# GpSimd's pauses between transfers left out from run 0B on, in a two-layer mixture-of-experts kernel

## The chip, the cores and the metric

The kernel runs on one core of one Trainium2 chip. The core has five engines with an instruction stream each: TensorE (PE in the profile, with PEld for its weight loads), VectorE (DVE), ScalarE (ACT), GpSimd (POOL) and SyncE (SP, which only starts transfers). What is measured is the device time of one execution in microseconds, lower is better. The same program is run several times and the median is taken.

## The reference, cut to what matters

2048 tokens (two sequences of 1024) of 256 numbers pass six layers, each added to x. The layers are a mixture of experts L0 (8 experts, 2 for each token, hidden width 176, and one shared expert), a time mix and a channel mix, the same L0 again, a mixture L1 (32 experts, 6 for each token, hidden width 96, and a shared expert), an attention whose sum runs over a whole sequence, and L1 again:

```
x = x + 0.5 * L0_ffn(layernorm(x))
x = x + L0_attn(layernorm(x))
x = x + 0.5 * L0_ffn(layernorm(x))
x = x + 0.5 * L1_ffn(layernorm(x))
x = x + L1_attn(layernorm(x))
x = x + 0.5 * L1_ffn(layernorm(x))

def _L1_ffn_ref(...):
    scores = jax.nn.sigmoid(x @ gate_w)
    topk_w, topk_i = jax.lax.top_k(scores, TOP_K)        # 6 of 32
    topk_w = topk_w / (jnp.sum(topk_w, axis=-1, keepdims=True) + 1e-20)
    ...
    act = jax.nn.silu(g) * u
    routed = jnp.einsum('tef,efd,te->td', act, wd, combine)
    shared = jax.nn.silu(x @ sg) * (x @ su) @ sd
    return routed + shared

def _L1_attn_ref(X, W_in, b_in, W_out, b_out):
    ...
    A = jnp.sum(feature_map(K) * V, axis=-2)             # over all 1024 tokens of a sequence
    Y = A[:, None, :] * Q
    ...
    return Y + X
```

## The kernel before, in words

**The mixture of experts.** The tokens stay in SBUF as 16 tiles of 128. A mixture does not run every expert on every token. For groups of four tiles it normalizes and scores the tokens (`prep`), and works out a slot for each pair of token and expert, so that the pairs of one expert fill whole blocks of 128 slots (`plan`). GpSimd then writes the normalized rows to their slots in DRAM: `scatter`, line 566, one indirect transfer of 128 rows for each tile and each choice (`xs`). Each block is loaded by SyncE (`fetch`, line 733), transposed, multiplied with its expert's weights (lines 764 and 781) and stored (`outward`, line 790, `ys`). Then GpSimd fetches each token's results back: `gather`, line 801, one indirect transfer for each tile and choice into one of eight buffers `yk`, and DVE adds it to x with its weight (`add_back`, line 813). A gather of a group waits for the stores of all blocks that the group can have (55 of them for the first group of a half, all of them for the second). A load waits for all scatters of its run.

**The order of the second half.** L1 runs on half A (tiles 0 to 7, the first sequence) and on half B (tiles 8 to 15), once before the attention and once after it, so there are four runs of blocks: 0A, 0B, 1A, 1B. Each has 68 blocks that are always there and up to 11 more under a condition. Each run has 48 scatters and 48 gathers. The attention over half A, with the gathers of 0A ahead of it and `prep`, `plan` and the scatters of 1A behind it, is written in between the blocks of 0B; for half B the same begins with the gathers of 0B. Shared experts (`shared`) fill places where no block is ready.

**The planner.** Each engine takes its instructions in a fixed order, so the order must be written out. `Clock` is a small planner that runs while the kernel is being built. Blocks advance its time (`BLOCK`, 1.41 us for a block of L1), and threads for gathers, scatters and attention (`clock.begin`) are resumed when their due time has come, whereupon they write out their next instructions. GpSimd has a clock of its own, `clock.pool`: each indirect transfer adds `CALL` = 1.27 us to it (line 317), and the next one is not written out before that time (`call`). Two threads that want GpSimd at one time are served by rank; gathers go ahead of scatters.

**The pauses.** After each third transfer, `called` (line 315) calls `pause` (line 325), as long as `pauses["on"]` is true. A pause is five memsets of a spare tile on GpSimd (lines 330 and 333), tied into order between the third transfer and the next one, and it adds `PAUSE` = 1.4 us to `clock.pool`. With the flag false, only the order is kept: the third transfer takes the memset's part as the one that the next transfers must follow (lines 322 and 323). In the kernel before, the flag becomes false at line 1515, when all blocks of 1B have been written out.

Of the kernel before, what the change touches and what calls it, by code (L numbers as in the profile page):

```python
# [55 lines left out]
def macaron_kernel(ctx: ExitStack, tc: tile.TileContext, a: dict, out: bass.AP):  # L56
# [248 lines left out]
    pauses = {"on": True}  # L305
# [806 lines left out]
    def wait(done):  # L1112
        while not done():
            yield clock.now + 1.0
# [171 lines left out]
    def all_of(part):  # L1286
        for us in part:
            clock.run(us)
# [36 lines left out]
    def pieces_of(part):  # L1325

        return dict(step=lambda: next(part, None), fetch_ahead=lambda: None)
# [103 lines left out]
    def second_pass(h):  # L1431

        added, result = set(), {}
        clock.begin(0, given_rows(m1[h], range(2), added))

        yield from wait(lambda: h in summed)
        yield from attend(h, moe_pool, added, result)
        m2[h] = half(
            1,
            h,  # L1440
            given=result["given"],
            out=out[HT * h * P : (HT * h + HT) * P, :],
        )
        for g in range(2):
            with behind_blocks():
                for t in range(BT * g, BT * g + BT):
                    result["out_of"](t)
            yield clock.spent(7.0, 8.0)
            yield from onward(m2[h], g, ready2[h])
        with behind_blocks():  # L1450
            m2[h]["owners"]()
            m2[h]["weights"](0)
        yield clock.now

    def sends(m, planned, sent, h, rank):
        for g in range(2):
            yield from wait(lambda: g in planned[h])
            yield from m[h]["scatter"](g, rank)
            sent[h].add(g)
# [36 lines left out]
    settle(lambda: 1 in sent1[1])  # L1496
    clock.begin(3, second_pass(1))
    clock.begin(2, sends(m2, ready2, sent2, 1, 2))
    part = m1[1]["shared"](0, HT)
    all_of(m1[1]["blocks"](lambda: pieces_of(part)))  # L1500
    all_of(part)
# [10 lines left out]
    clock.begin(5, given_rows(m2[1], range(2), done[1], 5))  # L1512
    part = m2[1]["shared"](0, HT)
    all_of(m2[1]["blocks"](lambda: pieces_of(part)))
    pauses["on"] = False
    all_of(part)
    settle(lambda: 1 in done[0], lambda: 1 in done[1])

# [52 lines left out]
```

## Time and profile before

| | |
|---|---|
| median of 7 runs | 1448.41 us (1445.52 to 1455.32) |
| the profiled execution | 1449.62 us |
| its span, first to last instruction | 1447.8 us |
| granted TensorE clock, mean | 0.898 |
| busy: PE, DVE, ACT, POOL | 1261.5, 735.2, 622.4, 667.8 us |
| pauses (memsets of line 330) | 157 |
| blocks of 0A, first and last `pg` matmul | 735.7 to 848.2 us |
| blocks of 0B | 849.3 to 1024.6 us |
| blocks of 1A | 1162.4 to 1272.0 us |
| blocks of 1B | 1272.9 to 1382.3 us |
| gathers of 0A, 0B, 1A, 1B, first and last start | 840.0 to 938.5, 986.2 to 1098.2, 1262.6 to 1358.3, 1372.9 to 1438.8 us |
| scatters of 1A, 1B | 1024.8 to 1156.4, 1157.7 to 1233.5 us |

The span is one execution as the hardware profiler recorded it. A line of the timeline gives the start in microseconds from the span's start, the duration, the engine, the line of the kernel, the operation and its tiles, and in brackets how long the engine had been idle before and what ended that idle time. In a table of stretches, each engine's busy time stands beside the number of its instructions; PEclk is the clock that the throttle granted to TensorE, as a share of full speed, and the DMA share is the mean busy share of the 16 DMA engines. A row of waits gives who waited for whom, the total in us, how often, and the longest.

### The profile page before, as it was taken

Reading aid. Unit: us, or ns where it says so; the run is one execution under the profiler, and the core shown is the slowest. Engines: PE = TensorE matmul, PEld = TensorE weight load, DVE = VectorE, ACT = ScalarE, POOL = GpSimd, SP = SyncE. Lnnn points to the kernel's source line nnn. Section 1 sums busy time; section 2 is a strip of 40 time slices with the busy share of each in tenths; the row PEclk is TensorE's granted clock in tenths of the full one; section 3 lists DMA queues with packets and bytes.
Section 4 is the critical chain, followed back from the end, with each engine's and each line's share of the span. In section 5 each row is a group of like instructions: output and inputs, shape, how many; then the busy total and the mean of one; then the engine's idle time right before and its main releaser. Section 6 shows DMA issues by size and latency. Waiting matters only on the chain. (4 is left out here: it accounts for less than half of the span.)

```text
span 1447.8 us, 23152 instructions
## 1 busy us (share of the span) xinstructions
PE 1261.5 (87%) x6100; PEld 967.2 (67%) x6100; DVE 735.2 (51%) x2507; ACT 622.4 (43%) x1671; POOL 667.8 (46%) x1346
## 2 busy tenths in 40 slices
PE   6599889889999789999979998988898799999970
PEld 4577657456666667766758987767655678977850
DVE  5333445856552432456454446764587354455653
ACT  4023553478664223442434545443323154544520
POOL 1630532001110550367777355505667777165475
PEclk9589889889999679989989999997789699999995
DMA  9723422990001823433667776533322267677743
GB/s 286 231 74 105 139 77 77 310 317 1 0 0 41 213 80 96 146 99 113 182 200 245 223 213 200 164 99 99 110 60 77 83 199 250 202 223 231 237 131 105
DMA packets 195170, 214.94 MB, mean 148 GB/s; under 512 B 40892, under 2 KB 178012, under 8 KB 195036
## 3 DMA queue, kind: packets, MB, share of 16 engines
q1 hardware_dynamic: 170460, 146.22, 32.8%
q0 software_dynamic: 24576, 67.14, 15.2%
q8 instruction: 59, 0.97, 0.3%
q14 instruction: 75, 0.61, 0.2%
HBM read 103.04 MB, written 110.23 MB: 147 GB/s over the span
## 5 line engine op out<-in xcount | busy, mean ns | idle before, releaser
L801 POOL DMA_INDIRECT yk_L<-ys_L,idx_L x64 | 62.3, 973 | 186.6 <-DMA ys_L<-yb_L 123.0
L333 POOL MEMSET still<- 128x96 f32 x628 | 112.7, 179 | 36.1
L764 PE MATMUL pg_L_b<-L0gu,xbT_L 128*128 x312 | 110.4, 479 | 0.0
L566 POOL DMA_INDIRECT xs_L<-xn_L,idx_L x64 | 62.0, 969 | 74.6 <-DMA xs_L<-zero 28.9
L659 PE MATMUL pg_L<-L0sgu,xTs_L 128*128 128x352 f32 x256 | 89.6, 484 | 2.6 <-DVE h_L L650 2.6
L801 POOL DMA_INDIRECT yk_L_0B<-ys_B,idx_L_0B x48 | 49.1, 1022 | 73.8 <-DMA xb_L_0B<-xs_B 46.7
L781 PE MATMUL py_L_b<-L0down,hT_L_b 88*128 x312 | 82.0, 385 | 0.0
L801 POOL DMA_INDIRECT yk_L_0A<-ys_A,idx_L_0A x48 | 46.2, 962 | 63.0 <-DMA xb_L_0A<-xs_A 28.0
L801 POOL DMA_INDIRECT yk_L_1A<-ys_A,idx_L_1A x48 | 46.0, 959 | 60.8 <-DMA ys_A<-yb_L_1A 28.1
L781 PEld LDWEIGHTS py_L_b<-L0down,hT_L_b 88*128 88x128 f32 x312 | 59.7, 194 | 20.0 <-issue 1.0
L764 PEld LDWEIGHTS pg_L_b<-L0gu,xbT_L 128*128 128x128 f32 x312 | 56.5, 199 | 20.1 <-issue 3.0
L650 DVE TENSOR_TENSOR h_L_b<-g_L_b,pg_L_b 128x176 f32<-128x176 f32 x78 | 26.3, 337 | 83.9 <-ACT g_L_b L649 72.0
L983 PE MATMUL pkk_cm<-mk_cm,w_WkeyT 128*128 128x512 f32 x128 | 62.7, 622 | 5.2 <-DVE mk_cm L975 3.5
L659 PEld LDWEIGHTS pg_L<-L0sgu,xTs_L 128*128 128x128 f32 x256 | 47.9, 199 | 25.4 <-DVE h_L L650 4.3
L764 PE MATMUL pg_L_0B_b<-L1gu,xbT_L_0B 128*128 x272 | 59.6, 345 | 2.4 <-DVEq L906 1.7
L801 POOL DMA_INDIRECT yk_L_1B<-ys_B,idx_L_1B x48 | 46.4, 966 | 29.3 <-DMA ys_B<-yb_L_1B 13.4
L764 PE MATMUL pg_L_1B_b<-L1gu,xbT_L_1B 128*128 x272 | 57.4, 334 | 2.9 <-ACT xbT_L_1B L746 1.4
L764 PE MATMUL pg_L_0A_b<-L1gu,xbT_L_0A 128*128 x272 | 57.6, 336 | 2.2 <-ACT g_L_0A_b L649 0.8
L995 PE MATMUL pkv_cm<-w_WvalT,sk_cm 128*128 128x256 f32 x256 | 58.0, 379 | 0.1
L764 PE MATMUL pg_L_1A_b<-L1gu,xbT_L_1A 128*128 x272 | 57.5, 335 | 0.3 <-DVE m_L_1B L193 0.2
L995 PEld LDWEIGHTS pkv_cm<-w_WvalT,sk_cm 128*128 128x128 f32 x256 | 48.3, 190 | 12.0 <-issue 5.0
L649 ACT ACTIVATE g_L_b<-pg_L_b 128x176 f32<-128x176 f32 x78 | 24.8, 318 | 73.2 <-PE pg_L_b L764 61.6
(639 smaller groups left out, 3387.0 us busy)
## 6 DMA issues: line engine op xcount, KB each, us to landing
xs_A<-zero SPq DMA_DIRECT2D x1, 10112.0 KB
xs_B<-zero SPq DMA_DIRECT2D x1, 10112.0 KB
xb_L<-xs_L SPq DMA_DIRECT2D x78, 128.0 KB
ys_L<-yb_L SPq DMA_DIRECT2D x78, 128.0 KB
xb_L_0A<-xs_A SPq DMA_DIRECT2D x68, 128.0 KB
ys_A<-yb_L_0A SPq DMA_DIRECT2D x68, 128.0 KB
xb_L_0B<-xs_B SPq DMA_DIRECT2D x68, 128.0 KB
ys_B<-yb_L_0B SPq DMA_DIRECT2D x68, 128.0 KB
```

The costliest lines, as they stand in the source:

```text
L333: d = nc.gpsimd.memset(still, 0.0)
L566: d = nc.gpsimd.indirect_dma_start(out=xs, out_offset=bass.IndirectOffsetOnAxis(ap=idx[:, t, k : k + 1], axis=0), in_=sent[g][t - BT * g], ...
L649: nc.scalar.activation(g, pg[:, 0:width], AF.Silu)
L650: nc.vector.tensor_tensor(dst, g, pg[:, width : 2 * width], ALU.mult)
L659: nc.tensor.matmul(pg, xbT[:, c, i * P : (i + 1) * P], w["sgu"][:, c, u, :, :].rearrange("p z w -> p (z w)"), start=(c == 0), stop=(c == D ...
L764: nc.tensor.matmul(pg, xbT[:, c, :], w["gu"][:, c, bass.ds(e, 1), :, :].rearrange("p e z h -> p (e z h)"), start=(c == 0), stop=(c == DC - 1),
L781: mm = nc.tensor.matmul(py, hT[0:HP, k, :], w["down"][:, bass.ds(e, 1), k, :].rearrange("p e d -> p (e d)"), start=(k == 0), stop=(k == C ...
L801: d = nc.gpsimd.indirect_dma_start(out=yk, out_offset=None, in_=ys[0 : n * P, :], in_offset=bass.IndirectOffsetOnAxis(ap=idx[:, t, k : k + ...
L983: nc.tensor.matmul(ps, w[:, c, oc * P : (oc + 1) * P], src[:, c, :], start=(c == 0), stop=(c == DC - 1),)
L995: nc.tensor.matmul(ps, src[:, c, i * P : (i + 1) * P], w[:, c, :], start=(c == 0), stop=(c == n - 1),)
```

## The change

The assignment that makes the flag false moves from behind the writing out of 1B's blocks to ahead of the writing out of 0B's blocks. By then the planner has written out the blocks of 0A and what its threads did beside them, the first gathers of 0A among it; all indirect transfers from there on follow each other without memsets, and without the 1.4 us on the planner's clock. Nothing else is edited.

```diff
     settle(lambda: 1 in sent1[1])
     clock.begin(3, second_pass(1))
     clock.begin(2, sends(m2, ready2, sent2, 1, 2))
+    pauses["on"] = False
     part = m1[1]["shared"](0, HT)
     all_of(m1[1]["blocks"](lambda: pieces_of(part)))
     all_of(part)
...
     clock.begin(5, given_rows(m2[1], range(2), done[1], 5))
     part = m2[1]["shared"](0, HT)
     all_of(m2[1]["blocks"](lambda: pieces_of(part)))
-    pauses["on"] = False
     all_of(part)
     settle(lambda: 1 in done[0], lambda: 1 in done[1])
```

## The prediction

> **What bounds the kernel now.** I read the page's engine line first: TensorE (PE) is busy 87% of a span of 1447.8 us, so a change on GpSimd (POOL) can only pay where PE runs short of work. To find those places I cut the second half at the borders of the stages, and read PE's busy time and granted clock of each stretch. The columns are the stretch, its length, busy time (and instructions) of PE, weight load, VectorE (DVE), ScalarE (ACT) and POOL, the clock, the DMA share and GB/s.
>
> ```profile
> 845.00:940.00 95.00, 86.53 (x471) 71.32 (x470) 60.02 (x179) 45.28 (x161) 56.72 (x120) 0.95 0.65 193
> 985.00:1024.00 39.00, 31.90 (x152) 27.20 (x152) 20.08 (x81) 12.85 (x34) 28.28 (x58) 0.74 0.37 106
> 1024.00:1050.00 26.00, 21.67 (x83) 16.09 (x82) 14.36 (x60) 9.83 (x20) 16.93 (x35) 0.75 0.29 100
> 1050.00:1100.00 50.00, 44.02 (x184) 28.71 (x183) 40.55 (x132) 14.78 (x40) 33.74 (x65) 0.89 0.22 62
> 1100.00:1161.00 61.00, 47.56 (x188) 35.55 (x187) 32.44 (x115) 16.79 (x34) 48.45 (x103) 0.77 0.24 86
> 1161.00:1272.00 111.00, 108.19 (x668) 94.89 (x669) 51.49 (x193) 56.41 (x210) 65.79 (x137) 0.97 0.70 220
> ```
>
> Runs 1A (from 1161) and 1B keep PE full at a clock of 0.97 and 0.98. Between 985 and 1161 it is not full: busy time by clock is 39.9 us of work in 65 us up to 1050 (31.90 x 0.74 + 21.67 x 0.75), and 75.8 us in the 111 us from 1050 to 1161 (44.02 x 0.89 + 47.56 x 0.77). So 25 and 35 us are there to be won. What ends the second of these stretches, in PE's timeline:
>
> ```profile
> 1153.12 4.46 PE L995 MATMUL po_at<-wA_at,axT_at 128*128 128x256 f32 x12
> 1161.21 1.11 PE L742 MATMUL px_L_1A<-ident,xb_L_1A 128*128 128x128 f32 x4 [3.63 <-DMA xb_L_1A<-xs_A]
> ```
>
> The first block of 1A waits for its load, and all loads of 1A wait for the last scatter of 1A. POOL's timeline shows what holds that up: the last scatter is issued at 1156.40, behind an unbroken row that began at 1049.81, when the blocks of 0B were done.
>
> ```profile
> 1049.81 0.98 POOL L801 DMA_INDIRECT yk_L_0B<-ys_B,idx_L_0B  x1 [4.55 <-SPq L906]
> ...
> 1152.87 0.96 POOL L566 DMA_INDIRECT xs_A<-axl_at,idx_L_1A  x1 [0.30 <-issue]
> 1153.82 0.20 POOL L330 MEMSET still<- 128x96 f32 x1
> 1154.08 0.89 POOL L333 MEMSET still<- 128x96 f32 x4
> 1155.13 0.97 POOL L566 DMA_INDIRECT xs_A<-axl_at,idx_L_1A  x1 [0.16 <-issue]
> 1156.40 0.96 POOL L566 DMA_INDIRECT xs_A<-axl_at,idx_L_1A  x1 [0.30 <-issue]
> ```
>
> The second place is the tail: after 1383 the chain that ended last is gathers of 1B and their adds, one per 1.25 us, and its first twelve gathers still had pauses:
>
> ```profile
> 1374.12 0.94 POOL L801 DMA_INDIRECT yk_L_1B<-ys_B,idx_L_1B  x1 [0.30 <-issue]
> 1375.06 0.20 POOL L330 MEMSET still<- 128x96 f32 x1
> 1375.32 0.89 POOL L333 MEMSET still<- 128x96 f32 x4
> 1376.73 0.95 POOL L801 DMA_INDIRECT yk_L_1B<-ys_B,idx_L_1B  x1 [0.52 <-DVE yb_L_1B L789]
> ```
>
> **What a pause costs.** Five memsets between two transfers. Between scatters, the gap from the end of one (1153.83) to the next start (1155.13) is 1.30 us against 0.30 without: 1.00 us. Between gathers it is 1.67 (1375.06 to 1376.73) against 0.30: 1.36, since a second semaphore wait (0.52) follows. The trace has 157 pauses; 83 come after 840. Four of the sixteen among the gathers of 0A belong to gathers written out while the blocks of 0A still were (group 0 is released 13 steps before their end, as in the tail, where twelve gathers got four pauses). So about 80 go: 12 in the gathers of 0A, 16 in those of 0B, 32 in the scatters of 1A and 1B, 16 in the gathers of 1A, 4 in those of 1B. No transfer is added. Each pause also took 1.4 us from the planner's own clock, so that gathers, adds, attention and scatters are written out earlier among the blocks on every queue.
>
> **Tail.** 4 x 1.36 = 5.4 us, on the path: nothing else of weight runs after 1400. The next thing that could be late is the second group's gathers, which need the last store of 1B; that was issued at 1390.0, and without pauses the 25th gather is due at 1372.9 + 24 x 1.25 = 1402.9. So −5.4.
>
> **The stretch from 1050 to 1161.** 20 pauses lie in it: 8 x 1.36 + 12 x 1.00 = 22.9 us. Eleven more lie between 986 and 1045; without them some 8 more scatters of 1A (ready from 1023) fit in before 1049.8, at 1.27 each another 10. The last scatter could go out 23 to 33 us sooner, and blocks of 1A could fill PE while attention over half B is still under way. The gain is no more than the 35.2 us that PE does not use here, and no less than the 3.6 us that PE waited for the load. That far apart, I take the middle, 19.4: attention itself starts 8 x 1.36 = 10.9 us sooner with its last gather, but its own waits (2.2, 2.5 and 2.3 us on DVE, 6.2 on ACT) stay and now stand inside PE's order. −19.4. What is late next is the rest of attention B, then the scatters of 1B; those were done at 1234, 38 us ahead of 1B's first block, so they stay covered. The 16 pauses among them cost nothing on the path, nor do the 16 among the gathers of 1A, over at 1358 with the tail's gathers waiting 13.4 us for block stores; without that cover the last would cost 21.8.
>
> **The stretch before 1050.** Twelve pauses of 0A's gathers are 16.3 us of POOL, and attention over half A hangs on them. But:
>
> ```profile
> POOL yk_L_0A L801 <- DVE x L813: 20.6, 9, 8.8
> ```
>
> POOL waited 20.6 us there for adds to free its buffers, more than the pauses cost. So anything between 0 and 16.3; I take a quarter, −4, nearer the row that says POOL was not the one to wait for.
>
> **What it costs.** While gathers run beside blocks, both share the DMA engines. Two stretches counted for the instructions of one tile alone (four matmuls of it to a block) show the price with pauses. The columns are as before, without POOL.
>
> ```profile
> 1236.00:1262.00 26.00, 15.19 (x76) 11.57 (x74) 4.57 (x18) 4.52 (x18) 1.00 0.64 192
> ...
> 1280.00:1355.00 75.00, 39.32 (x184) 29.52 (x184) 11.54 (x46) 11.35 (x45) 0.98 0.77 230
> ...
> DVE yb_L_1B L789 <- DMA ys_B<-yb_L_1B: 8.8, 6, 2.5
> ```
>
> Run 1A with no transfer from POOL: 19 blocks in 26 us, 1.37 each. Run 1B beside gathers: 46 in 75 us, 1.63 each, so 12 us lost (46 x 0.26), 8.8 of it in waits for stores. Without pauses three gathers take 3.77 us and not 5.12: denser by a third, and over sooner. If the loss goes with the time of overlap, it shrinks by a quarter, −3 in each of the two runs with gathers (0B and 1B); if it doubles with the density, +12 in each. No row shows unpaced gathers beside blocks; I take +4 each, +8, nearer no change, since the queue of GpSimd holds 28% of the engines in that part of 1B (1270 to 1320) and the other 49%, which a third more leaves under 90%.
>
> [...]
>
> **Sum.** −5.4 − 19.4 − 4 + 8 = −20.8 on the profiled execution's 1449.62 us (span 1447.8 and 1.8 around it): 1428.8. That execution lies 1.2 above the median of 1448.41, so 1428 for a median.
>
> **Rivals.**
> *It fills the hole.* All 35.2 us of the second stretch, 8 of the first, the tail, and a cost of 4: 1449.6 − 35.2 − 8 − 5.4 + 4 = 1405. For it: PE's order before 1161 has little that blocks could not stand beside. Against: attention over half A, among blocks, left PE at 86.53 of 95 us at 0.95, so even there 13 us stay open.
> *Moved, not won.* Attention B and not the scatters sets the start of 1B; PE gets only its 3.6 us, the tail 5.4, the cost takes 8: 1448.6. For it: the last matmul of attention ended at 1157.6, only 3.6 us before the block.
> *Slower: block transfers behind unpaced rows.* Place: the 16 rows of three beside each of 0B, 1A and 1B, 48 in all. Each transfer of GpSimd ahead of a load or store delays it; DVE then stands in front of the block's copy, and PE behind DVE. The point from which it decides is 28.8 us of gains by 48 rows, 0.6 us a row. At 0.9 us, twice one block transfer alone: 1449.6 − 28.8 + 43 = 1464. For it: the 8.8 us of store waits are there already, with pauses. Against: beside scatters, with pauses, PE was busy 108.19 of 111 us.
> That the pauses stay can't be: the flag is read at each third transfer.
>
> **Chances.** Forecast 0.45 (own range 1414 to 1443), hole filled 0.12, moved 0.13, slower 0.30. A measurement of this kernel tells some 0.3%, 4.3 us, from no change. Faster by more takes the forecast, the filled hole and a little of the third case, 0.60; same 0.10; slower 0.30. For eight in ten the range goes from the filled hole to the slower case, 1406 to 1464.
>
> **What would show it.** Right: 77 pauses left; the first block of 1A before 1140, its loads not waiting for the scatter; the clock from 1100 to 1161 above 0.9; the last gather ending 5 us closer behind the blocks. Wrong: 1.7 us or more for a block beside gathers; waits of block copies for stores far over 8.8 us; PE waits inside 1A on attention B's tiles as long as the hole was.

## The result: slower by 7.1%, and the profile after

The changed kernel takes 1554.19 us in the median of 18 runs (1543.17 to 1564.02), the kernel before 1451.59 us beside it. The ratio is 1.0711 [1.0692, 1.0729]. The forecast was 1428 us, and the range ended at 1464.

The flag does what it says: 78 pauses are left (312 memsets of line 333, four to a pause), where some 77 were expected. Nor does the DMA side show more load. From the page of the changed kernel, the row of the pauses and the two DMA queues (packets, MB, share of 16 engines over the span), and from its list of waits the copy that waits for stores:

```profile
L333 POOL MEMSET still<- 128x96 f32 x312 | 55.6, 178 | 17.8
...
q1 hardware_dynamic: 170460, 146.22, 30.6%
q0 software_dynamic: 24576, 67.14, 14.3%
...
DVE yb_L_1B L789 <- DMA ys_B<-yb_L_1B: 6.5, 5, 2.6
```

14.3% of 1554.5 us is 222 us of GpSimd's packets; before it was 15.2% of 1447.8, or 220. The waits for stores fell from 8.8 to 6.5 us. So the transfers take the same time, and no row of waits shows blocks that queue behind them. The loss is elsewhere. The stretches of the changed kernel, with the same columns as before:

```profile
1000.00:1070.00 70.00, 46.77 (x254) 38.66 (x253) 31.07 (x130) 19.78 (x58) 34.88 (x36) 0.76 0.34 112
1070.00:1171.00 101.00, 69.14 (x238) 43.42 (x237) 57.38 (x164) 26.02 (x67) 61.16 (x61) 0.84 0.29 90
1171.00:1369.00 198.00, 150.02 (x787) 129.03 (x786) 72.16 (x271) 69.18 (x227) 57.88 (x60) 0.77 0.40 127
1369.00:1492.00 123.00, 107.64 (x614) 92.08 (x613) 59.35 (x185) 51.25 (x204) 46.31 (x48) 0.96 0.69 202
```

The blocks of 0B last from 848 to 1066 us instead of from 849 to 1025. The first `pg` matmul of 1A starts at 1172 instead of 1162, and the blocks of 1A need 198 us instead of 111. In those 198 us PE has 48 us without work, DVE 126 and ACT 129: everybody waits. The timeline of one such place shows for whom. The number in brackets is the idle time before the instruction; "remote" there means that the profile names nobody who ended it:

```profile
1225.25 0.82 DVE L147 TENSOR_SCALAR axl_at<-x,rstd_L_1B,shift_L_1B 128x256 f32<-128x256 f32 x2
1225.71 1.97 PE L156 MATMUL pt_L_1B<-ident,axl_at 128*128 128x128 f32 x8 [6.62 <-issue]
1226.28 0.96 POOL L566 DMA_INDIRECT xs_B<-axl_at,idx_L_1B  x1 [0.30 <-issue]
1227.54 0.96 POOL L566 DMA_INDIRECT xs_B<-axl_at,idx_L_1B  x1 [0.30 <-issue]
1228.81 0.96 POOL L566 DMA_INDIRECT xs_B<-axl_at,idx_L_1B  x1 [0.30 <-issue]
...
1236.37 0.96 POOL L566 DMA_INDIRECT xs_B<-axl_at,idx_L_1B  x1 [0.30 <-issue]
1236.84 0.58 ACT L441 COPY axT_at<-pt_L_1B 128x512 f32<-128x512 f32 x1 [10.49 <-remote]
1237.63 0.96 POOL L566 DMA_INDIRECT xs_B<-axl_at,idx_L_1B  x1 [0.30 <-issue]
1238.94 0.58 ACT L441 COPY axT_at<-pt_L_1B 128x512 f32<-128x512 f32 x1 [1.52 <-remote]
```

PE issues eight transposes within 2 us. ACT copies their result, and nothing else is in its way, but its first copy starts 9 us later. ACT's copies wait for a semaphore that PE's matmuls raise, and the recording holds 1,718 changes of it as events with a time. They say the same: PE's three signals for these transposes come at 1234.71, 1236.81 and 1238.91, 2.1 us apart, where the matmuls were issued 0.21 us apart. During all of it GpSimd issues one scatter each 1.26 us without a break. Its row ends at 1238.6; the third signal still comes 0.8 us behind the matmul before it, and all of PE's signals in the next 20 us come within 0.014 us. The end of a matmul is modelled in these records, so they do not tell a late matmul from a late signal; below, "late signal" means either. Such a delay is nobody's busy time: here it stands in the 10.49 us that ACT is idle before its copy.

### The profile page after: what moved, and what is told of

Its sections match the earlier page's. It is cut to its first block, busy times and chain, and to the rows that moved or that the text cites. A ratio compares the mean times of both kernels' runs of the same rounds, so it can differ in the third digit from the quotient of the medians.

```text
span 1554.5 us, 22695 instructions
## 1 busy us (share of the span) xinstructions
PE 1285.7 (83%) x6100; PEld 982.7 (63%) x6100; DVE 735.9 (47%) x2507; ACT 623.9 (40%) x1673; POOL 596.5 (38%) x951
## 3 DMA queue, kind: packets, MB, share of 16 engines
q0 software_dynamic: 24576, 67.14, 14.3%
## 5 line engine op out<-in xcount | busy, mean ns | idle before, releaser
L801 POOL DMA_INDIRECT yk_L_1A<-ys_A,idx_L_1A x48 | 46.5, 969 | 102.2 <-DMA xb_L_1A<-xs_A 61.5
L566 POOL DMA_INDIRECT xs_A<-axl_at,idx_L_1A x48 | 47.2, 983 | 92.6 <-DVE idx_L_1A L557 78.3
L566 POOL DMA_INDIRECT xs_B<-axl_at,idx_L_1B x48 | 46.4, 966 | 79.3 <-DVE idx_L_1B L557 65.3
L764 PE MATMUL pg_L_0B_b<-L1gu,xbT_L_0B 128*128 x272 | 62.5, 357 | 3.6 <-issue 3.5
L764 PE MATMUL pg_L_1A_b<-L1gu,xbT_L_1A 128*128 x272 | 64.6, 367 | 0.3 <-issue 0.3
L333 POOL MEMSET still<- 128x96 f32 x312 | 55.6, 178 | 17.8
L650 DVE TENSOR_TENSOR h_L_1A_b<-g_L_1A_b,pg_L_1A_b 128x96 f32<-128x96 f32 x68 | 17.2, 253 | 89.6 <-ACT g_L_1A_b L649 54.2
```

Source lines behind the costliest of these rows:

```text
L333: d = nc.gpsimd.memset(still, 0.0)
L566: d = nc.gpsimd.indirect_dma_start(out=xs, out_offset=bass.IndirectOffsetOnAxis(ap=idx[:, t, k : k + 1], axis=0), in_=sent[g][t - BT * g], ...
L650: nc.vector.tensor_tensor(dst, g, pg[:, width : 2 * width], ALU.mult)
L764: nc.tensor.matmul(pg, xbT[:, c, :], w["gu"][:, c, bass.ds(e, 1), :, :].rearrange("p e z h -> p (e z h)"), start=(c == 0), stop=(c == DC - 1),
L801: d = nc.gpsimd.indirect_dma_start(out=yk, out_offset=None, in_=ys[0 : n * P, :], in_offset=bass.IndirectOffsetOnAxis(ap=idx[:, t, k : k + ...
```

## The experiments

### Two kinds of sessions

Nothing below can be read without one fact that came out on the way. Kernels that are measured together run in turns with the kernel before on one chip; I call this a session. The sessions were of two kinds, and all runs of one session agree.

```
session       kernel before, median   changed kernel
first         1451.59 us              1.0711 [1.0692, 1.0729]
chip 13       1430.35                 not run
chip 7        1431.72                 1.0043 [1.0012, 1.0074]
chip 2        1456.13                 1.0755 [1.0727, 1.0782]
chip 4        1433.02                 not run
chip 4 again  1451.33                 not run
chip 1        1461.67                 not run
chip 0        1430.64                 not run
```

Where the kernel before takes 1430 to 1433 us I call the session prompt, where it takes 1451 to 1462 us late. Chip 4 was prompt in one session and late in the next, five minutes on, so it is not the chip as such. In late sessions PE's signals come late beside transfers without pauses; in prompt sessions never. To count this, I took every event of the semaphore that PE's matmuls raise and its distance from the last matmul end before it, and called it late over 1 us (the first 60 and the last 100 us left out):

```
kernel                      session  signals  late  last transfer a scatter  a gather
before                      late       1497     0     0                       0
changed (first)             late       1599    51    23 ( 92.4 us)           28 ( 86.2 us)
changed (a3)                late       1616    79    26 ( 93.0 us)           51 (130.3 us)
no memsets, charged (g1)    late       1597    34    25 (128.9 us)            9 ( 20.9 us)
one memset (g2)             late       1618    56    19 (101.4 us)           32 ( 74.3 us)
gathers bare (h1)           late       1563    37     0                      37 ( 75.2 us)
scatters bare (h2)          late       1565    28    22 (114.4 us)            2 (  7.5 us)
no pause anywhere (e7)      late       1704   111    59 (320.1 us)           52 (108.7 us)
changed (a2)                prompt     1832     0     0                       0
no memsets, charged (e1)    prompt     1831     0     0                       0
scatters bare (e4)          prompt     1838     0     0                       0
gathers bare (e3)           prompt     1827     0     0                       0
```

The sums in brackets are of delays that partly overlap other work, so they are not a loss of time; the counts are what is to be read. (Signals without a transfer in the 5 us before are in the total alone: 2, 5 and 4 of a3, g2 and h2.) The other eight prompt recordings have no late signal either. It is PE's signals alone: in the first recording of the changed kernel the median of DVE's, ACT's and GpSimd's signals is 8 to 11 ns behind the end of an instruction, one of some 3,000 is late by over 1 us, and DVE and ACT are busy for 735.9 and 623.9 us, where before they were for 735.2 and 622.4.

One thing limits the counts. The recordings of late sessions are incomplete: of some 2,000 signals that PE's matmuls give they hold 1,612 to 1,823, and 11,800 to 12,600 events of DMAs that have landed, where prompt ones hold 1,986 to 1,996 and 21,200 to 21,300. So there may be more late signals than are counted, and in late sessions waits for a DMA are named less surely. The DMA packets are all there, some 195,180 in each.

### The changed kernel again

No edit, twice.

> The changed kernel itself, unaltered, beside the two below on one chip. In its first profile the completion signals of PE came late by 2 to 9 us for single matmuls in 1A (8 transposes issued within 2 us, their signals 2.1 us apart), and in none of the four kernels of the first batch. Theory A (it belongs to this order with bare rows): ratio 1.06 to 1.08 again, and late signals in the same stretches. Theory B (it belongs to the chip that the first profile came from): ratio 1.01 to 1.03, like the order alone with pauses (1.024), and no late signals.

Measured in a prompt session: 1.0043 [1.0012, 1.0074], 1438.22 us, and not one late signal. Theory B in this form (a chip) did not hold either, as chip 4 showed later, but the 7% does not belong to the program alone. The second time:

> The changed kernel unaltered once more: it gave 1.071 [1.069, 1.073] where it was first measured and 1.004 [1.001, 1.007] in the second place. Theory B1 (the 7% belongs to one chip or its state at that time): 1.00 to 1.01 on any other chip, 1.06 to 1.08 on that one, nothing between. Theory B2 (each chip has its own size of it): any value between 1.00 and 1.08, and the number of late signals of PE goes with it.

Measured in a late session: 1.0755 [1.0727, 1.0782], and late signals at many of the same matmuls, the transposes `pt_L_1A`, `pt_at` and `pt_L_1B` among them. So the two measurements are of one program, with the same instructions in the same order on PE, and a difference of 122 us in the span (1554.5 and 1432.2). Where it arises, as the start of the same matmul in the first session less that in the prompt one:

```
at (prompt)   675    825    975    1275    end
later by, us  1.1    6.0    17.1   102.6   122.3
```

Between 975 and 1275 it grows by 85.5 us; there the scatters of 1A and 1B (993 to 1221) run without pauses, and the gathers of 0B (1015 to 1091) too. The late signals can be set against it gap by gap. PE's 6100 matmuls stand in the same order in both recordings, and 26 gaps between two of them, those in which a late signal is recorded, hold 85 of the 122 us. (From e1 to g1 below, one program again, such gaps hold 71 of 111 us.) The rest is spread over small steps; part of it is the clock. In the 198 us of 1A, PE is busy for 150 us at a clock of 0.77, in the 143 us of the prompt session for 136 at 0.89, with nearly the same matmuls: of the 55 us between them 41 are idle time and 14 slower matmuls. The place of the stall above, in the prompt session:

```profile
1169.84 0.96 POOL L566 DMA_INDIRECT xs_B<-axl_at,idx_L_1B  x1 [0.30 <-issue]
1170.21 0.87 PEld L156 LDWEIGHTS pt_L_1B<-ident,axl_at 128*128 128x128 f32 x8 [2.69 <-DVE axl_at L147]
1170.22 1.11 PE L156 MATMUL pt_L_1B<-ident,axl_at 128*128 128x128 f32 x8 [2.28 <-DVE axl_at L147]
1171.10 0.96 POOL L566 DMA_INDIRECT xs_B<-axl_at,idx_L_1B  x1 [0.30 <-issue]
1171.25 1.07 ACT L441 COPY axT_at<-pt_L_1B 128x512 f32<-128x512 f32 x2 [0.42 <-PE pt_L_1B L156]
```

The same eight transposes inside the same kind of unbroken row, and ACT's copies start 1 us behind the first of them.

### Order and pauses taken apart

The change does two things: the memsets go, and the planner's clock runs ahead, which reorders the work of all engines. Theory 1 was that bare rows of scatters hold up the other engines' signals, theory 2 that the new order does it, theory 3 that bare rows starve the blocks' loads and stores.

e1 leaves the memsets out and charges the planner all the same:

```diff
                 else:
                     self.row.clear()
                     self.still = d.ins
+                    if pauses["charge"]:
+                        self.pool += PAUSE
...
+    pauses["on"] = False
     part = m1[1]["shared"](0, HT)
...
-    pauses["on"] = False
+    pauses["charge"] = False
     all_of(part)
```

Its order is nearly that of before: 87 of PE's 6100 matmuls stand in another place, where in the changed kernel 1295 do.

> From 0B's blocks on to the tail the memsets are left out, but the planner still adds 1.4 us for each pause to its own clock, so that the order of the work stays nearly that of before (a twentieth to a tenth of the reordering that the change makes). Theory 1 (an unbroken row of scatters on GpSimd holds up the completion signals of the other engines, whatever the order): slow like the changed kernel, 1520 to 1560 us, with PE nearly idle in rows of 20 and more scatters. Theory 2 (the uncharged planner writes scatters out ahead of attention, and GpSimd then stands at the head of its queue): as before or a little faster, 1430 to 1455 us. Theory 3 (block loads and stores starve behind bare rows of either kind): slow too, but with the waits on xb loads and ys stores, 1470 to 1560 us.

Measured (prompt): 0.9957 [0.993, 0.9985], with an unbroken row of 56 transfers from 1047 to 1123 us; PE is 90% busy beside its part from 1085 to 1114, 22 transfers of which 17 are scatters. That seemed to end theory 1. It was run again, twice, to separate the kinds of sessions:

> The same kernel as e1 (order nearly that of before, no memsets from 0B on), which gave 0.9957 where the kernel before takes 1430 us. Chips seem to be of two kinds: on some the kernel before takes 1430 us and the changed one 1.004 of it, on others 1451 to 1456 us and 1.071 to 1.076. On a chip of the first kind: 0.993 to 0.999 again. On one of the second kind: Theory 1 (bare rows hold up completion signals there, whatever the order): 1.05 to 1.08; Theory 2 (order): 0.99 to 1.005.

> The kernel of e1 and f1 (order nearly that of before, no memsets from 0B on). Where the kernel before takes 1430 us: 0.993 to 0.999, as twice. Where it takes 1450 us: Theory 1 (bare rows hold up PE's completion signals there, whatever the order) 1.05 to 1.08, with signals late by over 2 us in 1A; Theory 2 (it takes the new order too) 0.99 to 1.01, hardly a late signal.

Measured: f1 0.9957 [0.9929, 0.9984] (prompt), g1 1.0612 [1.0546, 1.0679] (late), both on chip 4. In a late session bare rows cost 6.1% in an order almost that of before: theory 1 holds there, if scatters and gathers are both taken for its rows, and the greater part of the 7% needs no new order. Theory 3 has little for it in a late session: in the stretch of 1A above the DMA share is 0.40, where the prompt session has 0.54, and no wait of a block for its load is listed there (with the reserve on named DMA waits made above).

e2 does the opposite: the memsets stay, and the planner is not charged from 0B on (`if pauses["charge"]:` ahead of `self.pool += PAUSE`).

> All the memsets of before are kept (those of the tail too), but from 0B's blocks on the planner charges nothing for them, so that the order of the work is nearly that of the changed kernel. Theory 1 (bare scatter rows hold up signals): near before, 1440 to 1470 us, and the stretches with PE under 40% in 1A are gone. Theory 2 (order): slow like the changed kernel, 1530 to 1565 us, with GpSimd waiting on idx at the head of its queue for over 60 us in a single wait. Theory 3 (starved block traffic): near before, 1440 to 1470 us.

> The same kernel as e2 (order of the changed kernel, all memsets kept), 1.024 on a chip of the first kind. On one of the second kind: Theory 1: 1.015 to 1.035, and no late signals of PE; Theory 2 (the order makes the 7%): 1.06 to 1.08.

> The kernel of e2 and f3 (order of the changed kernel, all memsets kept), 1.024 and 1.024 where the kernel before takes 1430 us. There again 1.02 to 1.03. Where it takes 1450 us: if bare rows make the late signals, 1.015 to 1.035 and no signal of PE late by over 1 us; if the order makes the 7%, 1.06 to 1.08.

Measured: 1.0241 [1.019, 1.0292], 1.0235 [1.0197, 1.0273] and 1.0197 [1.0156, 1.0238]. All three sessions were prompt, so what the order alone costs in a late one was not seen. In a prompt one it costs 2.0 to 2.4% if the pauses are kept. The order was written out for a faster GpSimd and is run by the slower one: in e2 the first block of 1A starts at 1164 us, not at 1123 as without memsets (in e5 below, with the order of before, at 1163), and the blocks of 1A then take 119 us, where in e5 they take 105.

### How long a stop must be

e6 is the changed kernel with one memset behind each third transfer:

```diff
                 else:
+                    with ExitStack() as st:
+                        for ins in self.row:
+                            st.enter_context(tc.issue_after(ins))
+                        d = nc.gpsimd.memset(still, 0.0)
                     self.row.clear()
```

> The order of the changed kernel (planner uncharged from 0B on), with one memset of 0.2 us behind each third transfer in place of five. With all five memsets the order gave 1.024, without any the change gave 1.071. Theory 1b (what stalls PE is a GpSimd that never lets go; any instruction between transfers lets the others through): 1.02 to 1.03. Theory 1c (what counts is the time per transfer, 1.27 us bare, 1.6 with five memsets): between, 1.04 to 1.07. Theory B (a property of the other chip): all three kernels of this order within 1.01 to 1.03.

> The same kernel as e6 (order of the changed kernel, one memset in place of five), 0.9967 on a chip of the first kind. On one of the second kind: Theory 1b (any instruction between the transfers lets the signals through): 0.99 to 1.03. Theory 1c (the delay goes with the time that GpSimd is given between transfers: one memset is a fifth of the pause): 1.04 to 1.07.

> The kernel of e6 and f2 (order of the changed kernel, one memset in place of five). Where the kernel before takes 1430 us: 0.995 to 1.00. Where it takes 1450 us: Theory 1b (any instruction between the transfers lets the signals through) 0.99 to 1.03; Theory 1c (the delay goes with the time given) 1.04 to 1.07.

Measured: 0.9967 [0.9937, 0.9997], below every range given, and 0.9977 [0.9949, 1.0005] (both prompt), 1.075 [1.0702, 1.0797] (late). A stop of one memset heals nothing where there is something to heal: 1.075 is the changed kernel's own 1.071 to 1.076. Theory 1b fell. Theory 1c gave 1.04 to 1.07, and the measured 1.075 lies above that: one memset was worth even less than a fifth, nothing that shows. k1 keeps three of the five, in nearly the old order (`range(4)` becomes `range(2)` from 0B on):

> From 0B on three memsets of the five, planner charged 1.4 us as before, so order near that of before. Where the kernel before takes 1430 us: 0.995 to 1.00 (none gave 0.9957). Where it takes 1450 us: if the stop's length counts in proportion, none 1.061, five 1.00, so 1.02 to 1.03; if it has a threshold over one memset's length, 0.99 to 1.00 or 1.05 to 1.07, by the side on which three lie.

Measured: 1.001 [0.9989, 1.003], but in a prompt session, slightly over what was expected there. Whether three memsets are enough in a late one stays open.

### Scatters and gathers apart

e3 keeps the pause of each row of three that ends on a scatter, e4 of each that ends on a gather (`called` is given the kind, and pauses if `pauses["kept"] == kind`).

> From 0B's blocks on only rows that end on a scatter keep their pause, gathers run bare; planner charged for the pauses that are there. Theory 1 (only unbroken scatters hold up signals): 1425 to 1460 us. Theory 2 (order, by the number of uncharged pauses, some half of 80): 1480 to 1520 us. Theory 3 (bare rows of either kind starve the blocks): 1480 to 1520 us.

> From 0B's blocks on to the tail only rows that end on a gather keep their pause, scatters run bare; planner charged for the pauses that are there. Theory 1 (unbroken scatters hold up signals): slow nearly like the changed kernel, 1510 to 1560 us. Theory 2 (order, by the number of uncharged pauses): 1480 to 1520 us. Theory 3 (bare rows of either kind starve the blocks): 1480 to 1520 us.

Measured (prompt): gathers bare 1.0023 [0.9985, 1.0061], scatters bare 1.0139 [1.0099, 1.018]. The 1.4% of the second has no late signals behind it; I have not traced it further. Again in a late session:

> The kernel of e3 (from 0B on rows that end on a scatter keep their pause, gathers run bare), 1.002 where the kernel before takes 1430 us. There again 0.998 to 1.006. Where it takes 1450 us: if the scatters do the harm, 1.00 to 1.02; if each bare row does, by its length, 1.025 to 1.045; if the gathers do it, 1.05 to 1.08.

> The kernel of e4 (from 0B to the tail rows that end on a gather keep their pause, scatters run bare), 1.014 where the kernel before takes 1430 us. There again 1.01 to 1.018. Where it takes 1450 us: if the scatters do the harm, 1.05 to 1.08; if each bare row does, 1.03 to 1.05; if the gathers do it, 1.01 to 1.03.

Measured: gathers bare 1.0242 [1.0213, 1.0271], scatters bare 1.0552 [1.0522, 1.0582]. Each kind does harm, scatters more, and the two together (2.4 and 5.5 points) come near the 7.1 to 7.6 of both. 1.4 points of the scatters' 5.5 and 0.2 of the gathers' 2.4 were there in a prompt session too, so what the late session adds is nearer 4.1 and 2.2. h1's 1.0242 lies just under the range for harm by each row's length, whose lower end its interval reaches; h2's 1.0552 lies in the range for harm by scatters. The table of late signals shows it without arithmetic: in h1 all 37 follow a gather, in h2 22 of the 24 that follow a transfer follow a scatter. A reason may be that a gather is held back by its eight buffers, so that GpSimd stops by itself (the prediction shows 20.6 us of such waits), which scatters of attention's rows have not (in the kernel before, none of the 96 of 1A and 1B waits longer than 0.3 us); no run tests this.

e7 has no pause anywhere, from L0 on (`pauses = {"on": False}`):

> No pause anywhere, planner uncharged from the start: 64 scatters and 64 gathers of L0 and all of 0A run bare too. Theory P (pauses are needed only where many transfers come unbroken beside blocks, and on a quiet chip nowhere): 0.985 to 1.005. Theory Q (bare scatters beside attention or L0's blocks hurt in themselves): 1.01 to 1.04. Where the changed kernel gives 1.07, this one gives at least 1.07.

Measured (late): 1.1655 [1.1628, 1.1682], as expected of a session in which the changed kernel gives 1.07, and far over theory Q's number. The longest delay of a signal was 14.5 us. In a prompt session it was not run. The head of its page:

```profile
span 1699.7 us, 22328 instructions
...
PE 1325.6 (78%) x6100; PEld 1007.6 (59%) x6100; DVE 735.4 (43%) x2507; ACT 629.5 (37%) x1677; POOL 523.8 (31%) x561
```

GpSimd is busy 144 us less than in the kernel before, and the kernel is 252 us longer.

### The last run alone

e5 makes the flag false ahead of 1B's blocks, where only gathers are left.

> The pauses go from the emission of 1B's blocks on, where no scatters are left: only gathers run bare. Nearest row: gathers alone bare from 0B on gave 1.002 [0.9985, 1.006]. Theory 1 (only scatters hurt, and only ahead of attention): 0.994 to 1.002. Theory 3 (bare gathers starve the blocks): 1.005 to 1.02, with 1B's blocks longer than 110 us.

Measured (prompt): 0.9992 [0.9966, 1.0018]. In a late session it was not run. No version was found that beats the kernel before in both kinds of sessions; the ones that beat it by 0.2 to 0.4% in a prompt one (e1, e6, each twice, one of the four intervals reaching 1) lose 6 and 7.5% in a late one.

## Why the prediction was wrong

**The step that failed** is "what it costs". It priced transfers without pauses by their share of the DMA engines alone, +8 us. In a late session the cost is not there: packets of GpSimd take as long as before (144 and 143 ns on average) and the waits for stores fell. What the bare rows cost comes, as far as it could be counted, from PE's late signals: the sum had +8, and measured against the kernel before in the same session the whole change lost 103 us. 85 of the 122 us between two executions of one program lie where a late signal is recorded. The prediction said that no row shows unpaced gathers beside blocks, and so bounded the cost by a neighbour of another kind. A bound from both sides would have had to allow for what five memsets every third transfer do besides taking time. The same holds for the sentence that the pauses among the scatters of 1B "cost nothing on the path": it asked what their removal saves and not what it may spoil, and scatters turned out the worse kind.

**The 19.4 us of the stretch before 1A** failed too, and this shows only where signals are prompt. The changed kernel's first block of 1A then starts at 1123 us, sooner than the 1140 that was to prove the step right, against 1163 in e5, which is the kernel before up to there. Both in prompt sessions, cut at the borders of their stages; first the changed kernel, then e5:

```profile
1031.00:1123.00 92.00, 69.83 (x255) 44.57 (x254) 61.94 (x177) 27.34 (x71) 66.79 (x67) 0.88 0.35 110
1123.00:1266.00 143.00, 136.45 (x783) 120.87 (x784) 69.09 (x265) 68.56 (x225) 54.26 (x56) 0.89 0.54 170
1266.00:1372.00 106.00, 99.72 (x616) 89.23 (x615) 60.28 (x186) 53.72 (x204) 46.83 (x49) 1.00 0.78 236
```

```profile
1026.00:1163.00 137.00, 113.10 (x448) 79.82 (x447) 86.34 (x303) 41.26 (x92) 99.19 (x200) 0.80 0.24 81
1163.00:1268.00 105.00, 104.58 (x666) 95.20 (x666) 52.19 (x193) 58.24 (x209) 64.65 (x136) 0.98 0.73 229
1268.00:1372.00 104.00, 100.89 (x616) 90.25 (x615) 61.68 (x189) 55.55 (x204) 50.53 (x62) 0.98 0.79 242
```

By busy time times clock, PE leaves 46.5 us open in e5's first stretch (137 − 113.10 x 0.80) and 2.5 in its second. In the changed kernel it leaves 30.5 and 21.6. So 49 us were open and 52 are. 1A begins 40 us sooner and ends 2 us sooner: attention over half B now stands among its blocks, in PE's fixed order, with the same waits. That is the rival "moved, not won", at 0.13; its 1448.6 is 0.999 of the profiled execution, and the prompt session gave 1.0043. The prediction took the middle between the ends 3.6 and 35.2. By the end of 1A its sum had won 19.4 us (−19.4, −4, and +4 for the blocks of 0B), and 2 at most is what came (1A ends 2 us sooner than in e5, but 0A had begun 2 us sooner already): the low end was right. The clock ahead of the first block of 1A, which was to be above 0.9, was 0.84 in the first measurement (1070 to 1171) and 0.88 in the prompt session.

**The 4 us before 1050** were not won either: in the prompt session the last gather of 0A starts 26 us sooner than in e5 (913.8 and 939.4), yet 0B's blocks end 5 us later (1031 and 1026).

**The tail**, −5.4, had the right sign and most of its size. From the last `pg` matmul to the end it is 62.5 us after 65.5 in the first measurement, and 60.4 in the prompt session against 63.7 to 64.7 with pauses kept (e2, f3, k2): 3 to 4 us.

**The rival "block transfers behind unpaced rows"** ended on the right side by luck, with the wrong mechanism. Its place was the 48 rows of three transfers beside the blocks of 0B, 1A and 1B and its price 0.9 us a row, by DMA, 43 in all. No run shows a row at that price; it is some twice the 0.42 us of all DMA engines that one block transfer took in the kernel before (61.7% of 32 us for 47 transfers, 1340 to 1372). Measured were 103 us net, scatters above all, and no queue that the rows of waits show. The count of `pg` matmuls of 1B beside the gathers of 1A shows it (PE's columns come first, the clock is the third number from the end). First the changed kernel in a prompt session, then in the first measurement:

```profile
1267.00:1326.00 59.00, 30.03 (x147) 22.66 (x145) 8.99 (x36) 9.24 (x37) 1.00 0.86 263
```

```profile
1370.00:1437.00 67.00, 31.29 (x145) 23.57 (x144) 9.03 (x36) 9.12 (x36) 0.95 0.75 222
```

Four to a block, that is 1.61 us for a block in the prompt session at a DMA share of 0.86. With pauses among the gathers, prompt runs show 1.72 in the same order (e2) and 1.52 and 1.54 in others (e4, k1). So bare gathers cost some 0.1 us a block there at most, 4 us for 37 blocks, which is what the prediction gave each run. In the late session a block takes 1.85 at a share of 0.75, and 1.64 in the kernel before at 0.78: what slows blocks there is not a fuller DMA. That the prediction's mark, 1.7 us or more for a block, is the price of bare gathers is shown by no run: 1.61 lies under it, 1.85 over it, and e2's 1.72 is with pauses.

Right were the number of pauses, and that a bare transfer takes 1.26 us.

## What to carry to other kernels

A stop that seems to waste an engine's time may hold something else in step (here, in late sessions, no signal of PE is late with five memsets after each third transfer, and 51 and 79 without), and a profile in which it always stands cannot price its removal by busy time; the honest range reaches to what its absence has never been seen to do. Work that is brought forward fills a hole only if what filled the time before it does not come along: add up the open time of both stretches, not of one (here 49 us were open, and 52 afterwards). And where a result and its repetition differ, put the two recordings of the same program side by side first: here that showed in one table that the order did not make the 122 us, and where they arose.

## What was not expected of the hardware

In late sessions the completions of PE come up to 14.5 us late while GpSimd issues indirect transfers of 128 rows each 1.26 us without a stop; five memsets after every third transfer prevent it (no signal late by over 1 us in the kernel before), and one does not. Even with the five, the kernel before takes 18 to 31 us more in a late session than in a prompt one. Set against two prompt recordings of nearly its order (e5 and k1), its late recording is level within 3 us at 1200, 10 to 13 us behind when the blocks of 1B end, and 15 to 16 at the end; the cause is open. In prompt sessions bare rows make no signal of PE late.

What makes a session late is open. The duration of packets is no sign of it: GpSimd's average 144.2 ns in the first recording of the changed kernel and 141.7 in the prompt one, and over all recordings 138.7 to 144.2 in late sessions and 141.3 to 143.9 in prompt ones. One thing goes with it in all recordings: those of late sessions hold 17,300 to 18,100 semaphore events, those of prompt ones 27,900 to 28,400, for nearly the same programs. Events are missing in the late ones, as said above; whether what loses them also delays PE's signals is not known. Each execution has a span and a clock on record, so no run here shows whether signals are late without a recording.
